# Attention's side work on VectorE: two steps in a unit that also has side work for the array, few in the others

## The chip, the cores and the metric

The kernel runs on one core of a Trainium2 chip. The metric is the device time of one execution in microseconds (us), the median of several runs. TensorE (PE) multiplies matrices into PSUM, VectorE (DVE) does reductions and elementwise work, ScalarE (ACT) exponentials and copies, GpSimd (POOL) elementwise work and indirect transfers, and SyncE (SP) starts most transfers. Each engine works through its own queue in order and waits for the others by semaphores.

## The reference

The input is x of shape (8, 1024, 256). Three layers follow each other, each added to x:

```
x = x + 0.5 * moe(layernorm(x))     # top-1 routing over 8 experts of 320 slots;
                                    # tokens past the slots go through one shared network
x = x + attention(layernorm(x))     # 16 heads of width 16, over 1024 positions
x = x + 0.5 * moe(layernorm(x))
```

Attention, which the change is about, computes for each batch and head

```
xd   = layernorm(x) @ W_down                    # split in 16 heads of 16
q, k, v = xd @ toqueries, xd @ tokeys, xd @ tovalues   (q and k scaled by 16 ** -0.25)
out  = softmax(q @ k.T) @ v                     # 1024 x 1024 scores for each head
x    = x + out @ W_unify + b_unify
```

## The kernel before

**Pairs and units.** The attention loop (`run`, from L1230) goes over 32 pairs n = 4 b + g: batch b of 8 and group g of four heads. A pair has 16 units u, two halves of the queries by eight blocks of keys. A unit is a fixed pattern on four engines:

- TensorE computes the scores of pair n (`psc`, L987, kinds "s" of `ORDERS`) into four PSUM banks and, interleaved with them and on other strips of the array, the scores of the next pair n + 1 the other way round (`pm`, also L987, kinds "m"), which use three PSUM banks.
- ScalarE turns the scores into exponentials (`ex`, L996), four instructions of 512 columns per unit. So the start of every fourth of them marks a unit.
- VectorE reduces each `pm` to its largest value (`halves`, L1003), four instructions per unit. These serve the next pair's softmax. Until a bank is reduced TensorE can't fill it again.
- TensorE multiplies the exponentials of the unit before by the values (`av`, L1018). After eight units VectorE transposes the sums and inverts the denominators (`turned`, `rec`, L1033 and L1036), GpSimd multiplies (`ot`, L1041), and after each second pair VectorE transposes back (`ho`, L1053). This falls into units 0, 1, 8 and 9. At the end of units 7 and 15 VectorE combines the maxima (L939 to L946), and SP carries them on (L948, L949).

**Side work.** Everything else in this stage is written as generators: `prepare(b)` (queries, keys and values of a coming batch: transposes L832, projections L862 and L880, values L894), `unify(b)` (the output projection L1063 and its addition to x, L1071), `stats(b)` (the attention norm of batches 4 to 7: eight pairs of L148 and L149, a closing part L151 to L160, and four Newton iterations L168 to L173, two to a step), `route(b)` (the same norm for the next layer, transposes, router logits L1091 and L1100, the places in the experts' slots in `places` L288 to L346, and eight sends to DRAM L184, L186, L361), and `biased(b)`. Each generator yields the kind of its next piece: `ARRAY`, `DVE` or `POOL`. They stand in a list `beside` with the pair by which they must be finished.

`step(kind)` takes one piece from the generator that is due first among those whose next piece is of this kind. `done_by(n)` at the end of a pair forces what is due by then. The order on TensorE, VectorE and ScalarE is exactly the order in which the Python code issues (`manual_schedule`); GpSimd and SP are ordered by the framework.

**Where pieces are taken.** Within each half of a pair, `SLOTS_OF` names the units (u modulo 8) for array pieces and those for VectorE pieces. In pairs with g of 2 or 3 array pieces are taken in units 0, 1 and 4 and VectorE pieces in 2, 3, 5 and 6; in pairs with g of 0 or 1 array pieces in 0, 1, 3 and 5 and VectorE pieces in 2, 4 and 6. So no unit has both. In a unit with an array piece (`other` is true) the whole `av` product comes before the second group of scores, and GpSimd's piece is left out.

Parts of `places` go back and forth: VectorE copies sums (L236), GpSimd adds three times (L238), VectorE adds (L308), GpSimd multiplies (L310), VectorE reduces (L312), and so on.

`queue(n)` puts new generators on the list at the start of a pair: for n of 1 to 4 also the load of batch 3 + n from DRAM (L74, after a one-element `memset` L1162) with its `stats`.

## Time and profile before

| | |
|---|---|
| median of 3 runs | 2935.99 us (2933.0 to 2938.25) |
| profiled execution | 2939.6 us, its span 2937.9 us |
| first layer, with the first pair's scores, to 662 us of the span | 662 us |
| attention loop | 662 to 2450 us, 1788 us |
| last layer | 2450 to 2938 us |
| busy in the span: TensorE, VectorE, ScalarE, GpSimd | 95%, 64%, 47%, 29% |
| mean granted TensorE clock | 0.981 |
| mean of one L1003, one L996 | 681 ns, 596 ns |

An instruction group in the profile is given as line, engine, operation, what it writes and reads, shapes, count, then its busy time and the mean time of one, then how long its engine had been idle before it and what it waited for. "<-PE pm L987" means that the wait ended when TensorE's `pm` at line 987 was done. In a list of stages the columns after the stage are its length, the busy time of PE, PEld (weight loads), DVE, ACT and POOL with their counts, the granted TensorE clock (1.00 is full), the busy share of the DMA engines and GB/s. In a timeline the columns are start, length, engine, line, operation and count; in brackets stands the idle time before it. Neighbouring instructions of one kind are merged there. The mean of L1003 includes overlap with the next one.

### The profile page before, as it was taken

Reading aid. Unit: us, or ns where it says so; the run is one execution under the profiler, and the core shown is the slowest. Engines: PE = TensorE matmul, PEld = TensorE weight load, DVE = VectorE, ACT = ScalarE, POOL = GpSimd, SP = SyncE. Lnnn points to the kernel's source line nnn. Section 1 sums busy time; section 2 is a strip of 40 time slices with the busy share of each in tenths; the row PEclk is TensorE's granted clock in tenths of the full one; section 3 lists DMA queues with packets and bytes.
Section 4 is the critical chain, followed back from the end, with each engine's and each line's share of the span. In section 5 each row is a group of like instructions: output and inputs, shape, how many; then the busy total and the mean of one; then the engine's idle time right before and its main releaser. Section 6 shows DMA issues by size and latency. Waiting matters only on the chain.

```text
span 2937.9 us, 56693 instructions
## 1 busy us (share of the span) xinstructions
PE 2799.3 (95%) x22066; PEld 1546.2 (53%) x22066; DVE 1883.1 (64%) x4189; ACT 1375.2 (47%) x2512; POOL 851.8 (29%) x1136
## 2 busy tenths in 40 slices
PE   4799999899999999999999999999999999999998
PEld 4567776454444444444444444444444445666775
DVE  7344223467897888888788788788788963212221
ACT  1111111207766666766766765766766663111111
POOL 3434433414001033123222321420420214432331
PEclk7799999999999999999999999999999999999999
DMA  7522553413112101301301301311321102321440
GB/s 224 152 83 78 176 187 99 161 47 121 53 58 97 67 24 60 124 24 56 128 24 52 133 24 42 125 41 39 125 80 38 39 3 73 128 61 49 150 147 28
DMA packets 163737, 251.47 MB, mean 86 GB/s; under 512 B 36737, under 2 KB 109698, under 8 KB 163458
## 3 DMA queue, kind: packets, MB, share of 16 engines
q1 hardware_dynamic: 144178, 196.93, 20.6%
q0 software_dynamic: 18432, 50.62, 5.1%
q8 instruction: 177, 2.90, 0.4%
q14 instruction: 102, 0.84, 0.1%
q10 hardware_dynamic: 848, 0.18, 0.0%
HBM read 144.10 MB, written 103.57 MB: 84 GB/s over the span
## 4 chain that ended last, share of the span: by engine, by line
PE 63%; DVE 13%; issue 1%; DMA 0%; POOL 0%; ACT 0%; POOLq 0%; DVEq 0%
PE psc L987 20%; PE av L1018 15%; DVE halves L1003 9%; PE pm L987 6%; PE pe_o L499 5%; PE ph_o L456 5%; PE pe_e L499 2%; PE ph_e L456 2%; PE pu L1063 2%; PE pxd L862 2%; PE pv L894 1%; DVE turned L1033 1%; PE pq L880 1%; PE pl L1091 1%; PE ptrn L832 0%
## 5 line engine op out<-in xcount | busy, mean ns | idle before, releaser
L1003 DVE TENSOR_REDUCE halves<-pm 128x1 f32<-128x512 f32 x2048 | 1309.3, 681 | 260.9 <-PE pm L987 239.6
L996 ACT ACTIVATE ex<-psc 128x512 f32<-128x512 f32 x2048 | 1111.4, 596 | 574.5 <-PE psc L987 570.9
L987 PE MATMUL pm<-k,q 32*128 32x512 f32 x4096 | 870.5, 448 | 50.6 <-DVE halves L1003 38.6
L987 PE MATMUL psc<-q,k 32*128 32x512 f32 x4096 | 791.8, 455 | 3.1 <-PEq L668 3.1
L1018 PE MATMUL av<-ex,vp 128*32 128x256 f32 (+1 forms) x6472 | 610.9, 449 | 0.0
L987 PEld LDWEIGHTS psc<-q,k 32*128 32x128 f32 x4096 | 326.6, 183 | 479.0 <-issue 423.1
L987 PEld LDWEIGHTS pm<-k,q 32*128 32x128 f32 x4096 | 374.9, 183 | 133.4 <-DVE halves L1003 107.3
L987 PE MATMUL psc<-m,ones_r 32*128 32x512 f32 x2048 | 406.9, 390 | 0.0
L456 PE MATMUL ph_o<-bT_o,oa 128*128 128x512 f32 x704 | 318.6, 601 | 7.1 <-DVE h_o L474 5.3
L499 PE MATMUL pe_o<-ob,h_o 128*128 128x256 f32 x1408 | 322.6, 386 | 0.0
L1041 POOL TENSOR_TENSOR ot<-turned,rec 128x256 f32<-128x256 f32 x64 | 39.7, 620 | 883.9 <-DVE rec L1036 875.6
L499 PEld LDWEIGHTS pe_o<-ob,h_o 128*128 128x128 f32 x1408 | 268.1, 193 | 48.5 <-issue 13.8
L1018 PEld LDWEIGHTS av<-ex,vp 128*32 128x32 f32 x6472 | 127.6, 108 | 298.3 <-issue 275.6
L456 PEld LDWEIGHTS ph_o<-bT_o,oa 128*128 128x128 f32 x704 | 131.2, 191 | 159.7 <-issue 147.4
L470 ACT ACTIVATE h_o<-ph_o,ob 128x512 f32<-128x512 f32 x88 | 60.5, 687 | 328.9 <-PE ph_o L456 305.0
L987 PEld LDWEIGHTS psc<-m,ones_r 32*128 32x128 f32 x2048 | 196.6, 184 | 13.0
L474 DVE TENSOR_SCALAR h_o<-ph_o,ob 128x512 f32<-128x512 f32 x88 | 65.9, 748 | 196.2 <-ACT h_o L470 179.4
L509 DVE SCALAR_TENSOR_TENSOR y_o<-pe_o,old_o 128x256 f32<-128x256 f32 x88 | 37.2, 423 | 205.8 <-PE pe_o L499 141.2
L499 PE MATMUL pe_e<-wb,h_e 128*128 128x256 f32 (+1 forms) x640 | 143.9, 381 | 0.0
L456 PE MATMUL ph_e<-bT_e,wa 128*128 128x320 f32 x512 | 140.6, 433 | 1.8 <-ACT bT_e L204 1.8
L204 ACT COPY bT_o<-pt_bT_o 128x1024 f32<-128x1024 f32 x22 | 22.3, 1012 | 250.8 <-PE pt_bT_o L200 225.9
L499 PEld LDWEIGHTS pe_e<-wb,h_e 128*128 128x128 f32 (+1 forms) x640 | 112.9, 179 | 16.4 <-issue 3.1
(183 smaller groups left out, 2385.1 us busy)
## 6 DMA issues: line engine op xcount, KB each, us to landing
k<-krows SPq DMA_DIRECT2D x64, 512.0 KB
wa<-in_w_dram SPq DMA_DIRECT2D x16, 1024.0 KB
wb<-in_w_dram SPq DMA_DIRECT2D x16, 1024.0 KB
krows<-kh SPq DMA_DIRECT2D x32, 512.0 KB
krows<-kl SPq DMA_DIRECT2D x32, 512.0 KB
q<-qrows SPq DMA_DIRECT2D x32, 512.0 KB
rows_o<-buf SPq DMA_DIRECT2D x88, 130.0 KB
x<-in_x_dram SPq DMA_DIRECT2D x8, 1024.0 KB
```

The source lines that it names most:

```text
L456: nc.tensor.matmul(ps[:, i * 512 : i * 512 + width], lhsT=wa[:, k, (m + i) * P : (m + i + 1) * P], rhs=xnt[:, k, c0:c1], start=(k == 0), s ...
L470: nc.scalar.activation(t[:, 0, : hi - lo], ps[:, lo - c0 : hi - c0], AF.Relu, bias=bias[:, m : m + 1],)
L474: nc.vector.tensor_scalar(t[:, 1, : hi - lo], ps[:, 512 + lo - c0 : 512 + hi - c0], bias[:, m + 1 : m + 2], 0.0, ALU.add, ALU.max,)
L499: nc.tensor.matmul(ps[lo - i * P : hi - i * P, :D], lhsT=of[:, lo - a : hi - a], rhs=w[:, m, :], start=(m == 0), stop=(m == MC - 1),)
L509: nc.vector.scalar_tensor_tensor(y[:n, :], ps[:n, :D], 0.5, olds[i][:n, :], ALU.mult, ALU.add)
L862: nc.tensor.matmul(ps, lhsT=wd_sb[:, k, m * P : (m + 1) * P], rhs=xnt[:, k, :], start=(k == 0), stop=(k == KC - 1),)
L987: nc.tensor.matmul(ps, lhsT=lhs, rhs=rhs, start=(len(left) + 1 == todo[kind, h, "of"]), stop=not left,)
L996: nc.scalar.activation(ex, ps, AF.Exp, scale=S ** -0.5)
L1003: nc.vector.tensor_reduce(halves[m][:, t, half, h : h + 1], ps, AX.X, ALU.max, negate=True)
L1018: nc.tensor.matmul(avs[n, q][32 * h : 32 * h + 32, cols], lhsT=vps[b % 2][:, at : at + 2 * S], rhs=ex[:, cols], start=(c == 0), stop=(c == ...
L1041: nc.gpsimd.tensor_tensor(outs_t[q][:, :, at : at + S].rearrange("p (t a) s -> p a t s", t=4), by[:, :, :S].rearrange("p (a t) s -> p a t ...
L1063: nc.tensor.matmul(ps[:, i * D : (i + 1) * D], lhsT=outs[b, g, q][:, at : at + P], rhs=wu_sb[:, g, :], start=(g == 0), stop=(g == G // 2 - 1),
```

## The change

`SLOTS_OF` keeps only the units for array pieces, unchanged. The units for VectorE pieces are no longer listed. Where an array piece is taken in a unit, two VectorE pieces are taken right after it. In the other units one VectorE piece is taken only in the seventh of each half (u modulo 8 of 6), and in the last pair, which has no next pair, in each odd unit.

```diff
-        SLOTS_OF = [((0, 1, 4), (2, 3, 5, 6)), ((0, 1, 3, 5), (2, 4, 6))]
+        SLOTS_OF = [(0, 1, 4), (0, 1, 3, 5)]
...
-                        other = u % TB in slots[0] and due(ARRAY) is not None
+                        other = u % TB in slots and due(ARRAY) is not None
...
-                    if u % TB in slots[1]:
+
+                    if other:
+                        step(DVE)
+                        step(DVE)
+                    elif u % TB == TB - 2 or not ahead and u % 2:
                         step(DVE)
                     if not other:
                         step(POOL)
```

An array piece counts as taken also where the generator only ends there and issues no matmul. The order of the pieces within a generator is the same as before, and so are all instructions.

## The prediction

> **What bounds the kernel now.** I read the page first (busy shares, costliest groups), then the busy time by stage, then who waited for whom in attention, then VectorE's timeline at the places that the change touches.

> ```profile
> PE 2799.3 (95%) x22066; PEld 1546.2 (53%) x22066; DVE 1883.1 (64%) x4189; ACT 1375.2 (47%) x2512; POOL 851.8 (29%) x1136
> ...
> L1003 DVE TENSOR_REDUCE halves<-pm 128x1 f32<-128x512 f32 x2048 | 1309.3, 681 | 260.9 <-PE pm L987 239.6
> ```
> ```profile
> 662.00:2450.00 1788.00, 1746.50 (x17698) 808.71 (x17693) 1462.77 (x2894) 1207.10 (x2244) 426.89 (x527) 1.00 0.19 65
> ```
> ```profile
> DVE halves L1003 <- PE pm L987: 214.1, 471, 4.0
> ...
> PEld pm L987 <- DVE halves L1003: 92.1, 145, 1.3
> ```
> Attention is 1788 us: TensorE is busy 1746 of them, VectorE 1463. VectorE waits 214 us for TensorE's scores and TensorE's weight loads wait 92 us for VectorE's reductions, so TensorE leads and VectorE follows so closely that any lump on it shows. 92 us is more than this change could give back, since the fixed work of units 0, 1, 8 and 9 causes part of it.

> A unit's length is the distance between the starts of every fourth `ex` (L996). The plain unit, with neither array work nor a step, is 2.94 us. VectorE's four reductions start 0.605 us apart, so they fill 2.42 of it and leave 0.26 behind each pair of them.

> **What a step costs today.** A half iteration is three Newton operations (L168, L169, L173), and a step holds two halves:
> ```profile
> 1242.12 1.29 DVE L1003 TENSOR_REDUCE halves<-pm 128x1 f32<-128x512 f32 x2 [0.17 <-PE pm L987]
> ...
> 1246.39 0.16 DVE L168 TENSOR_TENSOR a_f<-yi_f 128x8 f32<-128x8 f32 x1
> ...
> 1247.38 0.17 DVE L173 SCALAR_TENSOR_TENSOR yn_f<-a_f,yn_f 128x8 f32<-128x8 f32 x1
> 1247.47 2.58 DVE L1003 TENSOR_REDUCE halves<-pm 128x1 f32<-128x512 f32 x4
> ```
> ```profile
> 1245.48 1.09 ACT L996 ACTIVATE ex<-psc 128x512 f32<-128x512 f32 x2 [0.54 <-PE psc L987]
> ...
> 1249.07 1.09 ACT L996 ACTIVATE ex<-psc 128x512 f32<-128x512 f32 x2 [1.07 <-PE psc L987]
> ```
> The six operations hold VectorE 1.08 us, and the unit that the step runs into lasts 1249.07 - 1245.48 = 3.59 us instead of 2.94: some 0.63 lost. A statistics step (L148, L149) holds it 0.55 and costs 0.09. Both fit one rule, an estimate: loss = holding - cover - 0.20, where the cover of a plain unit is 0.26 and 0.20 is the lead that TensorE has through its three `pm` banks.

> In a unit with array work, the cover, VectorE's idle time before the next reduction, is 1.53 us (projection, L862, L880), 1.59 (values, L894), 0.91 (transposes, L832), 0.5 (router logits, L1091), 1.0 (projection in unit 0 or 8). It is nothing with `unify`, whose own addition waits for the matmuls:
> ```profile
> 1564.52 0.69 DVE L1071 TENSOR_TENSOR x<-x,pu 128x512 f32<-128x512 f32 x1 [0.44 <-PE pu L1063]
> 1565.13 0.20 DVE L946 STREAM_TRANSPOSE lowturned<-lowboth 128x32 f32<-128x32 f32 x1
> 1565.26 1.24 DVE L1003 TENSOR_REDUCE halves<-pm 128x1 f32<-128x512 f32 x2
> ```

> **The change, part by part.** I wrote out from the code which step falls into which unit, before and after. No instruction is added; the order moves.

> *Routes 0 to 5.* Before, a route is spread over pairs 4k+1 to 4k+4. After, its statistics fall two at a time into units 0, 1, 3, 5 of pair 4k+1 (score and value projections, transposes), both Newton steps into unit 8, transposes and logits into pair 4k+2, the slot chain into units 0 and 1 of pair 4k+3. Taken away per route: two Newton steps at 0.63, four statistics at 0.09: 1.6 us. Placed: two statistics hold 1.1, under the idle times above: 0. Two Newton steps hold 2.16 in unit 8 with a cover of 1.09: 2.16 - 1.09 - 0.20 = 0.87. `top` to `chosen` in one unit waits for POOL's L293 (0.32, with hand-overs 0.5): 0.39 + 0.5 + 0.39 held, 0.58 covered: 0.5. The last step before them, alone: 0.1. The chain:
> ```profile
> 1776.76 0.20 DVE L236 COPY sums<-places 128x56 f32<-128x56 f32 x1
> 1778.19 0.22 DVE L308 TENSOR_TENSOR place<-sums,places 128x64 f32<-128x64 f32 x1 [1.23 <-POOL sums L238]
> ```
> VectorE is held 1.6 us here with POOL's three additions. Then POOL's L310 (0.65 with hand-overs), L312 to L316 (0.5) and L321 (0.25) follow in the same unit 0: 3.0 in all; unit 1 gets 1.2 + 0.63 for `behind` and the slots. With the division's work (1.2) and eight reductions (4.84) VectorE needs 10.8 for two units in which TensorE has 7.0. They take about 10.7. Spread as before they cost 9.35 (units 0 and 1: 6.82; added by the two array steps and what follows: 1.62 and 0.91). Price 1.4. In return the transposes in units 0 and 8 cover the division's delay (3.63 instead of 2.94 there): -0.8. Per route -1.6 + 0.87 + 0.5 + 0.1 + 1.4 - 0.8, with up to 0.2 because a prepare step sits one slot earlier, is +0.5; six routes: +3.

> *Norms of batches 4 to 7 (`stats`).* Taken away: 7.0 us (units 3.0 to 3.7 long in pairs 1, 2, 3, 6, 7, 10). Placed: pair 4 has `unify`, so nothing covers: two statistics 0.95 and (behind `ho`) 1.1, final step and Newton 1.37, Newton and statistics 1.36; unit 8, where the generator only ends, 1.1; 0.7 after: 6.6. Pair 1, unit 8 also has no matmul: 2.3 for two Newton steps. Pairs 5 and 6: 0.7 and 2.6 (logits with two Newton steps and the 0.7 of `ho`). Single steps elsewhere: 0.4. Together 12.6.

> Then a wait that did not exist. The load of batch 4 is issued at 720.39 on SP, behind two loads of `k` and one of `q`; before, its first reader came at 731.78:
> ```profile
> 722.40 1.22 DVE L1003 TENSOR_REDUCE halves<-pm 128x1 f32<-128x512 f32 x2
> 723.53 0.20 DVE L946 STREAM_TRANSPOSE lowturned<-lowboth 128x32 f32<-128x32 f32 x1
> 724.39 1.29 DVE L1003 TENSOR_REDUCE halves<-pm 128x1 f32<-128x512 f32 x2 [0.65 <-PE pm L987]
> ...
> 731.78 0.42 DVE L148 BATCH_NORM_STATS2 st_a<-x 128x6 f32<-128x256 f32 x1
> ```
> After, it stands at 723.6 at the head of VectorE's queue, with L946, the pair's reductions and so TensorE behind it (and SP's L948, `krows` behind L946; their readers are eight units away). The trace's packets of this load end at 728.11, its semaphore seems complete at 728.4. [...] I take 5.0. Stats net: 12.6 + 5.0 - 7.0 = +10.6.

> *Route 6 and the end.* Before, its Newton steps and transposes lie in pairs 29 to 31 and only slots and sends are left at 2450. After, it gets four steps by pair 30, the rest in pair 31, where VectorE is nearly idle; transposes come in the last unit. Taken away: 4 us. Left over, one behind the other: copies, POOL's second rows (4 x 1.22), transposes, logits, two POOL hand-overs, slots: 16.8 us against 5. Upper end 12. The lower end is about 0: at the border of the sections TensorE took L200 of the next layer ahead of the last `pu` groups, so part may be filled. I take 8: net +4.

> *POOL.* Sends (1.22 + 0.19 + 1.1) move to units 2 to 9 of pair 4k+3, one per 2.94: tight, `ot` may come 2 us late; `ho` is read a unit later. Zero; up to 0.5 per route if not.

> *Clock.*
> ```profile
> 1775.50:1779.10 3.60, 3.45 (x33) 1.62 (x28) 2.32 (x6) 2.17 (x4) 1.56 (x5) 1.00 0.00 0
> 1779.10:1782.50 3.40, 3.40 (x25) 1.51 (x25) 2.27 (x6) 1.09 (x2) 0.20 (x1) 0.50 0.00 0
> ```
> A slot chain is followed by 3.4 us at half clock; that unit took 5.10 instead of 3.61. It happened twice in attention. [...] I take 4.

> Sum: 3 + 10.6 + 4 + 4 = 21.6, bounds +1 to +40. The profiled execution took 2939.6 (span 2937.9), 3.6 above the median 2935.99; the gain or loss is set on the median: 2957.

> **The rivals.** *Faster (9%):* the idle times do cover, because VectorE's lag is carried over several units instead of stopping TensorE. For it: 1.5 us in some 30 units. Then takings of 1.6 x 6 + 7 + 4 = 20.6 remain against the load wait and half the rest, 9: 2924. It decides at a lead of about a microsecond; against it stands 0.09 for a 0.55 us step, a lead of 0.20. *No change (9%):* the order does not do what it says in most batches. In pairs 4k from 8 on there are seven array units and no VectorE step is ready. If then the end is filled and no clock window falls, about +4: 2940. *Far slower (20%):* end wholly exposed, eight half-clock windows, late `ot`: 2936 + 36 = 2972. *Forecast (62%):* 2942 to 2966, 2957 likeliest.

> A difference of 0.2%, 5.9 us, is about what a measurement of this kernel can tell from none. The range leaves out most of the two upper rivals' far ends: 2936 to 2975. Slower 0.82, within 0.09, faster 0.09.

> **What would show it.** Right: a wait of L148 for the load of `x` near 724 of 4 to 6 us; pair 4 at 66 us instead of 59.9; units 0 and 1 of pair 4k+3 together near 10.7; pairs 2, 3 and 30 shorter by 1.6 to 2.6; a gap on TensorE after 2450. Wrong: weight loads waiting for L1003 well under 92 us in all, or no load wait. Pairs 4k+1 longer than 61 us would mean that the lead is smaller than I read.

## The result and the profile after

The kernel after takes 3003.52 us (median; 2999.3 to 3006.52), the kernel before 2937.12 with the runs made beside it: ratio 1.0226, 95% interval 1.0209 to 1.0244. The change costs 66 us. The direction was forecast, the size (21 us) was not, and the time lies above the range.

The page of after first: busy time, share and instructions of each engine, then VectorE's group of reductions (busy, mean ns, idle time before them).

```profile
PE 2850.3 (95%) x22122; PEld 1573.7 (52%) x22122; DVE 1894.5 (63%) x4189; ACT 1374.9 (46%) x2512; POOL 851.9 (28%) x1136
...
L1003 DVE TENSOR_REDUCE halves<-pm 128x1 f32<-128x512 f32 x2048 | 1312.0, 682 | 292.8 <-PE pm L987 279.4
```

VectorE works as long as before (1895 against 1883 us), but TensorE is busy 51 us longer with the same matrices (its count is higher because the trace of before lacks 56 more of their records). That is the first hint: TensorE ran slower for part of the time. Next the two stages, after the first layer (window; then busy us of PE, PEld, DVE, ACT and POOL; granted clock, DMA share, GB/s):

```profile
664.20:2498.00 1833.80, 1777.50 (x17686) 817.78 (x17687) 1471.94 (x2881) 1203.04 (x2237) 418.74 (x512) 0.98 0.18 63
2498.00:3003.00 505.00, 482.98 (x1965) 340.20 (x1957) 125.20 (x316) 73.32 (x121) 177.60 (x241) 0.97 0.29 91
```

The mean clock in attention fell from 1.00 to 0.98. And within attention (waits of one line for another: us in total, times, longest):

```profile
DVE halves L1003 <- PE pm L987: 254.3, 651, 2.9
PEld pm L987 <- DVE halves L1003: 113.3, 166, 4.5
```

Both waits grew, VectorE's by 40 us and TensorE's by 21: VectorE is still the follower, and each has become the other's obstacle more often. Units are compared by the starts of every fourth `ex`. From the first `ex` to the last the loop lasts 1786.5 us before and 1835.0 after; what follows it lasts 489.2 and 503.6. TensorE's time at half clock within the loop is 11.0 us before and 85.3 after.

**The forecast wait for the load of `x`** (VectorE's timeline, start and length; in brackets the idle time and its releaser):

```profile
727.54 1.22 DVE L1003 TENSOR_REDUCE halves<-pm 128x1 f32<-128x512 f32 x2
733.40 0.43 DVE L148 BATCH_NORM_STATS2 st_a<-x 128x6 f32<-128x256 f32 x1 [4.64 <-DMA x<-after_first]
...
734.49 0.18 DVE L946 STREAM_TRANSPOSE lowturned<-lowboth 128x32 f32<-128x32 f32 x1
```

L946 and with it the reductions stand behind it. The unit lasts 11.49 us instead of 4.67; 6.83 us of half clock follow from 733.6 on.

**A kept bank, which nobody forecast.** In pairs 4k+2 of after, units 2, 3, 10 and 11 last 3.80 us, although no piece is in 2 and 3 but VectorE's usual work. Pair 18, on TensorE, TensorE's weight loads and VectorE:

```profile
1726.74 1.06 PE L1091 MATMUL pl<-rw,Trn 128*128 128x8 f32 x8
1738.14 1.06 PE L1091 MATMUL pl<-rw,Trn 128*128 128x8 f32 x8
```
```profile
1729.87 0.18 PEld L987 LDWEIGHTS pm<-k,q 32*128 32x128 f32 x1 [0.42 <-DVE halves L1003]
1731.77 0.18 PEld L987 LDWEIGHTS pm<-k,q 32*128 32x128 f32 x1 [0.41 <-DVE halves L1003]
1733.67 0.18 PEld L987 LDWEIGHTS pm<-k,q 32*128 32x128 f32 x1 [0.42 <-DVE halves L1003]
```
```profile
1739.24 0.18 DVE L1100 TENSOR_TENSOR logits<-pl,rb 128x32 f32<-128x32 f32 x1
```

The router's products go into `pl`, a bank of the same pool of three that `pm` uses. The first piece writes it at 1726.7, the second at 1738.1, and only L1100 at 1739.2 lets it go. For some 12.5 us `pm` has two banks; each half of a unit lasts 1.90 us instead of 1.47, and the weight loads wait 0.4 us for a reduction each time. Before, the two pieces lay in adjacent units (0 and 1, 8 and 9 of pairs 4k+3): in pair 19 they start 4.2 us apart, and L1100 comes 5.3 us after the first. The order of array pieces changed nowhere in the code; the route is simply ready for them one pair earlier, where the array's units are 0, 1, 4.

**Half clock, here after a slot chain** (pair 23; window, busy times as above, clock):

```profile
2013.60:2017.00 3.40, 2.58 (x24) 1.50 (x28) 2.63 (x6) 1.08 (x2) 0.81 (x5) 1.00 0.05 9
2017.00:2027.30 10.30, 10.11 (x72) 3.93 (x69) 5.63 (x12) 4.34 (x8) 8.26 (x12) 0.50 0.14 48
```

Three windows of 3.41 us at half clock follow one in which TensorE was without a recorded product for only 0.8 us. The granted clock recorded in this trace is 1.0 or 0.5, and all its changes, from 126.05 to 2993.25 us, lie on one grid of 3.41333 us, to within 0.002 us; in the trace of before, from 24.64 to 2929.38 us, they lie on one of the same spacing, to within 0.001 us. The loop has eleven stretches at half clock, of one to four windows: 10.2 us at its start (pair 0; before 4.1), 6.8 behind the wait for the load, 13.6 behind Newton steps of the attention norms (pairs 1, 4 and 6), 20.5 behind pieces of the router's products (pairs 6, 10 and 14) and 34.1 behind slot chains (pairs 15, 23 and 27). Behind the slot chains of pairs 7, 11 and 19 there is none.

**The end.** Route 6 finishes alone (VectorE's timeline):

```profile
2509.38 0.19 DVE L1100 TENSOR_TENSOR logits<-pl,rb 128x32 f32<-128x32 f32 x1 [3.40 <-PE pl L1091]
...
2513.37 0.22 DVE L308 TENSOR_TENSOR place<-sums,places 128x64 f32<-128x64 f32 x1 [1.22 <-POOL sums L238]
...
2517.16 0.17 DVE L343 TENSOR_TENSOR slot<-row,behind 128x8 int32<-128x8 f32 x1 [0.32 <-POOL behind L342]
```

The first product of the next layer's experts (`ph_o`) starts at 2520.5, before at 2456.1. That is 64.4 us later, of which 50.5 are already there at the end of the loop.

### The profile page after: what moved, and what is told of

Read it like the earlier page. It is cut to its first block, busy times and chain, and to the rows that moved or that the text cites. A ratio compares the mean times of both kernels' runs of the same rounds, so it can differ in the third digit from the quotient of the medians.

```text
span 3002.8 us, 56812 instructions
## 1 busy us (share of the span) xinstructions
PE 2850.3 (95%) x22122; PEld 1573.7 (52%) x22122; DVE 1894.5 (63%) x4189; ACT 1374.9 (46%) x2512; POOL 851.9 (28%) x1136
## 4 chain that ended last, share of the span: by engine, by line
PE 61%; DVE 14%; issue 1%; POOL 1%; DMA 1%; ACT 0%; POOLq 0%; DVEq 0%; ACTq 0%
PE psc L987 20%; PE av L1018 14%; DVE halves L1003 9%; PE pm L987 5%; PE pe_o L499 5%; PE ph_o L456 5%; PE pe_e L499 2%; PE ph_e L456 2%; PE pu L1063 2%; PE pxd L862 1%; PE pv L894 1%; PE pq L880 1%; DVE turned L1033 1%; PE pl L1091 1%; PE ptan L832 0%
## 5 line engine op out<-in xcount | busy, mean ns | idle before, releaser
L1003 DVE TENSOR_REDUCE halves<-pm 128x1 f32<-128x512 f32 x2048 | 1312.0, 682 | 292.8 <-PE pm L987 279.4
L996 ACT ACTIVATE ex<-psc 128x512 f32<-128x512 f32 x2048 | 1111.3, 596 | 622.7 <-PE psc L987 620.4
L987 PE MATMUL pm<-k,q 32*128 32x512 f32 x4096 | 882.3, 455 | 65.2 <-DVE halves L1003 50.5
L987 PE MATMUL psc<-q,k 32*128 32x512 f32 x4096 | 810.8, 461 | 3.0 <-PEq L668 3.0
L1018 PE MATMUL av<-ex,vp 128*32 128x256 f32 (+1 forms) x6528 | 623.4, 454 | 0.0
L987 PEld LDWEIGHTS psc<-q,k 32*128 32x128 f32 x4096 | 331.4, 186 | 497.0 <-issue 412.8
L987 PEld LDWEIGHTS pm<-k,q 32*128 32x128 f32 x4096 | 378.4, 187 | 147.5 <-DVE halves L1003 128.6
L987 PE MATMUL psc<-m,ones_r 32*128 32x512 f32 x2048 | 412.9, 395 | 0.0
L987 PEld LDWEIGHTS psc<-m,ones_r 32*128 32x128 f32 x2048 | 200.4, 188 | 13.8
```

What stands on the lines that cost most here:

```text
L987: nc.tensor.matmul(ps, lhsT=lhs, rhs=rhs, start=(len(left) + 1 == todo[kind, h, "of"]), stop=not left,)
L996: nc.scalar.activation(ex, ps, AF.Exp, scale=S ** -0.5)
L1003: nc.vector.tensor_reduce(halves[m][:, t, half, h : h + 1], ps, AX.X, ALU.max, negate=True)
L1018: nc.tensor.matmul(avs[n, q][32 * h : 32 * h + 32, cols], lhsT=vps[b % 2][:, at : at + 2 * S], rhs=ex[:, cols], start=(c == 0), stop=(c == ...
```

## The experiments

Times are medians; ratios, with their 95% intervals, are to the kernel before on the same chip (medians of 2936.5 to 2941.8), and can differ by 0.2% from the quotient of two medians. "Half" is TensorE's time at half clock within the loop (11.0 before, 85.3 after), in the one execution that was profiled. Executions of one kernel differ by up to some 25 us (before_wide: 2958.09 to 2983.39), so a single value of it says little about a few microseconds of the median. A unit or pair is said to be at full clock when no half clock lies in it.

### One cause at a time

**The slot chain spread again: one VectorE step instead of two in pairs 4k+3** (after_chain_apart)

```diff
                     if other:
                         step(DVE)
-                        step(DVE)
+                        if n % G != 3:
+                            step(DVE)
```

> The changed kernel with one VectorE step instead of two in array units of pairs 4k+3 only, so that L321 and the second array piece of the slot chain go to units 6 and 8. Theory 2, the chain of slot steps through VectorE and GpSimd in one unit stops TensorE long enough that the clock is halved for some 10 us: units 0 to 2 of pairs 4k+3 fall from 13.5 us together to about 11.5 and what leaves comes back partly in unit 8; the half-clock windows in pairs 4k+3 and just before go away: 3003.5 to about 2985. Rival 2, the clock windows come from elsewhere (the kept bank in pairs 4k+2, or chance): gain of at most 6, windows as many as before (75 us of the loop).

2982.54, ratio 1.0155 (1.0131 to 1.0179): 21 us better than after. Pairs 4k+3 last 52.6 us (53.2 at full clock in after), only some 4 us in all; half fell to 39.3. Between the profiled executions the loop is 18.9 us shorter, most of it clock; the first layer, which the edit does not touch, is 7.0 shorter too.

**No step in units 0 to 2 of pair 1** (after_load_first), so that nothing asks for the `x` of batch 4 before it has come

```diff
                     if other:
-                        step(DVE)
-                        step(DVE)
+                        if n != 1 or u > 2:
+                            step(DVE)
+                            step(DVE)
```

> The changed kernel without VectorE steps in units 0 to 2 of pair 1, so that no statistics stand at the head of VectorE's queue before batch 4 has come from DRAM. Theory 4: the wait of 4.64 us and the half-clock time behind it (10 us) leave pair 1, which goes from 65.3 to 57 to 58 us; pair 4 and later pairs take on the steps that are put off, within 2 us: 3003.5 to about 2996. Rival 4: the stop of TensorE in pair 1 has another cause, pair 1 stays above 62.

2996.4, ratio 1.0179 (1.0155 to 1.0203). Pair 1 lasts 56.2 us, without half clock, instead of 65.3: the load wait cost 9 there, of which its own 4.64 us are half. The loop as a whole was only 1.5 us shorter in the profiled execution (the slowest of four), since other pairs had more half clock (half 89.3).

**The kernel before's VectorE slots from pair 28 on** (after_end_old)

```diff
-                    if other:
+                    if n >= (B - 1) * G:
+                        if u % TB in ((2, 3, 5, 6), (2, 4, 6))[n % G < 2]:
+                            step(DVE)
+                    elif other:
...
```

> The changed kernel with the VectorE slots of the kernel before in the last four pairs (28 to 31), the new rule elsewhere. Theory 3, the end: route 6 is no longer left for after the loop; the stretch from the loop's end to the kernel's end is 490 us again instead of 505, pairs 28 to 31 lose their gain of 5.5: 3003.5 to about 2994. Rival 3: the 14 us behind the loop are clock or chance: no change beyond 3.

2985.64, ratio 1.0175 (1.0131 to 1.0218): 18 us better than after, where 10 were expected. What follows the loop lasts 489.4 instead of 503.6, with 8.3 us of half clock in it instead of 26.6. So the late end is real and worth some 14 us, part of it clock; the rest of the 18 is not the end's (in the profiled execution the untouched first layer is 4.8 shorter).

**The logits read later in the kernel before: a bank kept without any other change** (before_logits_late)

```diff
+                for _ in range(2 - q):
+                    yield DVE
                 nc.vector.tensor_tensor(
                     logits[:, 4 * q : 4 * q + 4, :],
...
-                yield ARRAY if q == 0 else DVE
+                if q == 0:
+                    yield ARRAY
```

> The kernel before with only the reading of `pl` (L1100) put off: for the first four rows by two VectorE slots (from unit 1 to unit 3 of pairs 4k+3), for the second by one (unit 9 to 10, together with L289 and L291). No steps in pairs of two, no other piece moves. Theory 1, the kept bank: units 2, 3 and 10 become 3.80 instead of 2.92 us, 2.6 us a route, six routes in the loop 15.6: about 2952. Rival 1: a late reader costs nothing but two empty steps: 2937 within 2.

2962.84, ratio 1.0076 (1.005 to 1.0102). Units 2, 3 and 10 of pairs 4k+3 last 3.80 instead of 2.92, as forecast; half rises to 21.1, which was not expected and makes 3 to 4 of the 11 us above the expectation; some 6 lie outside the loop and are not explained. The kept bank alone costs 0.86 us a unit, in a kernel that is otherwise before.

### The kept bank taken away, and the gain that did not come

**All of the router's products in the first piece** (after_pl_whole), **or all in the second** (after_pl_together)

```diff
-                    if i == 1:
-                        yield
```
```diff
+                yield
                 pl = bank_v(f"pl_{b}_{q}")
...
-                    if i == 1:
-                        yield
```

> The changed kernel with both halves of the router logits (L1091) of four rows in one array piece, so that the PSUM bank `pl` is not kept from one array piece to the next. Theory 1, the kept bank: in the changed kernel `pl` is written in units 1 and 9 of pairs 4k+2 and released only in units 4 and 12, and TensorE has two `pm` banks instead of three meanwhile; units 2, 3, 10 and 11 then go back from 3.80 to about 2.94 us, pairs 4k+2 lose 3.6 us or more, six routes 22 us: 3003.5 to about 2979. Rival 1, VectorE lags from the steps taken two at a time, or GpSimd's adds and row norms slow VectorE: units 2, 3, 10, 11 stay near 3.8 and the time stays within 3 us of 3003.

> The changed kernel with the first of the two array pieces of the router logits left empty and all eight products in the second, so that every piece keeps its unit and only the time that `pl` is kept shrinks. Theory 1, the kept bank: units 2, 3, 10 and 11 of pairs 4k+2 fall from 3.80 to 2.94 us, units 4 and 12 grow by what the products take (under 0.9); pairs 4k+2 from 56.9 to about 53.5 us where no half clock falls into them, 6 x 3.4 = 20 us: 3003.5 to about 2983, give or take 8 for the clock. Rival 1 (lag of VectorE, or GpSimd beside it): pairs 4k+2 stay above 56.

3002.13 (1.0218; 1.019 to 1.0247) and 3005.93 (1.0197; 1.0165 to 1.0228). No gain. Yet the units did what was expected: 2 and 3 are back at 2.94 in the one, pair 22 is at 54.2 us in the other. Instead half rose to 119.5 and 123.5. In after_pl_whole the slot chain also moves, into pairs 4k+2, of which those from 10 on hold 13 to 27 us of half clock each; in after_pl_together pairs 4k+3 with their slot chain hold 6 to 14.

**Twelve products of 384 columns (not used) behind each of the slot chain's two groups of products, added to after_pl_whole** (whole_filled), to keep TensorE streaming there

```diff
             nc.tensor.matmul(total, lhsT=ones_r, rhs=chosen, start=True, stop=True)
+            for _ in range(12):        # and the same behind the products of "behind"
+                nc.tensor.matmul(ps[:, 128:512]..., lhsT=ones_r, rhs=ones_r..., ...)
```

> As after_pl_whole (both halves of the router logits in one piece), and besides twelve matmuls of 384 columns that nobody reads behind the matmuls of `places` and twelve behind those of `behind` (L304 to L331), so that TensorE has 2 us of work in each of the two places where it waits for the slot chain; their output is not used. Theory 2, halted TensorE halves the clock: the half-clock time in the attention loop falls from 119 us to under 50 and the kernel gets faster by 15 to 25 us although it does more work: about 2980. Rival 2, the clock does not follow the halts in the chain: half-clock time stays near 119 us and the time stays at 3002 or grows by up to 2 x 2 us a route, 3002 to 3026.

3024.14 (1.0273; 1.0247 to 1.03). They lengthened the chain more than they filled it; half fell only from 119.5 to 90.4. This decides nothing.

### What brings half clock

**One or two reductions of 2048 elements on VectorE (not used), in ten plain units of the kernel before** (before_hold_2: one; before_hold_4: two)

```diff
+                    if n % G == 0 and 8 <= n < 28 and u % TB == 6:
+                        for i in range(1):        # 2 in before_hold_4
+                            hold = small.tile([P, 8], F32, tag="hold", ...)
+                            nc.vector.tensor_reduce(
+                                hold, bu_sb.unsqueeze(1).to_broadcast([P, 8, D]), AX.X, ALU.max
+                            )
                     last = (n, u, [todo["ex", h] for h in range(4)])
```

> The kernel before with one reduction of 2048 elements of SBUF on VectorE (result not used) in units 6 and 14 of pairs 8, 12, 16, 20 and 24, which had neither array work nor a step: ten halts. The reduction holds VectorE about 2.1 us, so by holding less cover (0.26) less lead (0.20) each costs 1.65: 16 us in all, 2953, with pairs 4k at 62.5. If a halt of TensorE also brings half clock, 3.4 us or more of it follow each halt, and the pairs with it are longer by 0.35 of its time: 3.4 us at each would add 12 us, 10 us at each 35 us. If it does not, the loop stays at 11 us of half clock.

> As the kernel with one reduction, with two of them in each place: VectorE is held about 4.2 us, and by holding less cover less lead each halt costs 3.75: 38 us in all, 2975, pairs 4k at 66.8. TensorE then stands still for more than one window of 3.4 us, so half clock is to follow nearly every halt: ten times 3.4 to 10 us, 12 to 35 us more. If the length of a halt decides, this kernel shows far more half clock than the one with one reduction; if only the phase decides, about the same.

2972.21 (1.0101; 1.0066 to 1.0136) and 3009.55 (1.0233; 1.0201 to 1.0264). The reduction holds VectorE 2.28 us. In before_hold_2 two of the five pairs show no half clock: they are 4.5 and 3.6 us longer, 1.8 to 2.2 for each hold, and the prediction's rule (holding less 0.26 less 0.20) gives 1.82. The other three have 4.9, 8.2 and 10.9 us of half clock and are 5.3, 6.5 and 7.8 us longer. Less the mean 4.02 that leaves 0.27, 0.31 and 0.35 us lost for each us of half clock (0.33 to 0.35 with the half clock that runs over into the next pair). In before_hold_4 all ten holds are followed by it.

Which halts it follows is seen when the time is cut in windows of 3.41 us, counted from a change of the clock. Twice the same hold (before_hold_2, pairs 12 and 8; columns as above):

```profile
1368.57:1371.98 3.41, 1.93 (x26) 0.99 (x25) 3.40 (x5) 1.26 (x3) 0.00 (x0) 1.00 0.00 0
1371.98:1375.39 3.41, 3.41 (x23) 1.04 (x20) 2.43 (x8) 1.25 (x3) 0.00 (x0) 0.50 0.00 0
```
```profile
1133.06:1136.47 3.41, 2.68 (x32) 1.03 (x29) 3.35 (x5) 2.17 (x4) 0.00 (x0) 1.00 0.08 25
1136.47:1139.88 3.41, 2.12 (x25) 0.99 (x25) 3.36 (x7) 1.09 (x2) 0.00 (x0) 1.00 0.01 2
1139.88:1143.29 3.41, 2.67 (x30) 1.14 (x28) 3.34 (x9) 2.17 (x4) 0.62 (x1) 1.00 0.02 5
```

In pair 12 the halt falls into one window: TensorE streams 1.93 of 3.41 us, and the next window is at half clock. In pair 8 it is shared by neighbours, 2.12 is left, and nothing follows. The six windows of this kernel behind which the holds brought half clock had 1.83 to 2.15 us of busy TensorE; holds that brought none left 2.00 or more. So holds of one length, 2.28 us, differ here by how the windows cut the halt; with two of them in a place, half clock followed at all ten.

**Products of 8 columns against products of 384 columns** (before_narrow, before_wide), in the same ten units, none of them used

```diff
+                    if n % G == 0 and 8 <= n < 28 and u % TB == 6:
+                        fill = bank_v(f"fill_{n}_{u}")
+                        for _ in range(16):       # before_wide: 12
+                            nc.tensor.matmul(fill[:, :8], ...)   # before_wide: 384 columns
```

> The kernel before with 16 products of 8 columns each (result not used) on TensorE in units 6 and 14 of pairs 8, 12, 16, 20 and 24, ten places, as the router's products stream them: some 1.95 us each, 20 us in all. If TensorE counts as busy in them, nothing else changes: 2957 and 11 us of half clock in the loop. If products of 8 columns count as standing still, a window of 3.41 us that holds 1.4 us of them is followed by half clock: some seven of the ten places, 35 us or more of half clock, 12 us more, 2969.

> The same places with 12 products of 384 columns each (result not used), some 2.0 us in each place, 20 us in all. If what counts is what TensorE streams, no half clock follows any of the ten places: 2957 and about 11 us of half clock in the loop. If any disturbance of the order brings half clock, it shows as much of it as the kernel with the narrow products.

3007.07 (1.0227; 1.0209 to 1.0245) and 2969.47 (1.0101; 1.0069 to 1.0133). The narrow ones came out longer than meant, 3.7 us and more a place (each product is two instructions), the wide ones 2.36 at the first place. Around the first place, narrow and then wide:

```profile
1130.99:1134.40 3.41, 3.41 (x38) 2.78 (x32) 1.80 (x4) 1.09 (x3) 0.00 (x0) 1.00 0.10 33
1134.40:1141.22 6.82, 6.82 (x47) 4.00 (x46) 2.29 (x4) 1.62 (x4) 0.00 (x0) 0.50 0.01 2
```
```profile
1134.11:1137.52 3.41, 3.41 (x34) 2.64 (x30) 1.46 (x4) 0.73 (x3) 0.00 (x0) 1.00 0.00 0
1137.52:1140.93 3.41, 3.41 (x44) 1.38 (x36) 3.16 (x9) 2.65 (x6) 0.00 (x0) 1.00 0.01 2
```

By the record TensorE is busy throughout in both. Half clock follows all ten places of the narrow products and none of the wide ones (half 102.4 and 24.6; in before_wide it lies in pairs 0 and 11). So half clock follows these products of 8 columns as it follows the halts above. The narrow work was also the longer; but TensorE had no gap in it, so length alone explains nothing. Not separated is whether the few columns matter or the weight load ahead of each of the 32 instructions (12 in the wide ones).

That is part of what ate the gain of the single piece: it puts 1.95 us of such products next to each other. Most of the rest fell behind the slot chain and the work around it. With products of 8 columns left out of the count, half clock followed, over the traces of all 18 kernels, 67 of 75 full-clock windows of the loop in which TensorE was busy under 1.7 us, 69 of 143 with 1.7 to 2.3, 41 of 1963 with 2.3 to 3.3, and none of 7068 with more. Counted as busy, these products would leave 62 windows with more than 3.3 us that half clock followed. Of the 41, 30 hold products of the slot chain: why it follows these at up to 3.3 us of recorded work stays open.

**The two pieces in adjacent units** (after_pl_near): array pieces in units 0, 3, 4 of pairs 4k+2

```diff
-                    slots = SLOTS_OF[n % G < 2]
+                    slots = (0, 3, 4) if n % G == 2 else SLOTS_OF[n % G < 2]
```

> The kernel after, with its array steps in units 0, 3, 4 and 8, 11, 12 of pairs 4k+2 (0, 1, 4 before), so that the two pieces of the router's products come in adjacent units, as in the kernel before, and not in one burst. If the kept bank is the cost, two units less per half of a pair last 3.80 instead of 2.94: pairs 4k+2 from 56.9 to about 53.5 at full clock, 20 us in all, and no half clock is added: 2983. If half clock comes from disturbances of any kind, it rises as it did with the single piece, and the time stays at 3000 or above.

2981.73, ratio 1.0138 (1.0116 to 1.016), near the forecast of 2983, though by another sum: pairs 18, 22 and 26 last 54.1 to 54.3 us instead of 56.8 to 56.9, 2.7 us a pair or 16 in all where 20 were expected, and half falls to 58.6, some 8 us more. Pairs 4k+2 hold only 3.4 us of half clock, in pair 6. So the bank's cost was real, and with the single piece its gain had been spent on the clock.

### Put together

**The four single edits at once** (after_mended: all products in the second piece, one step in pairs 4k+3, no step in units 0 to 2 of pair 1, old slots from pair 28), **and one Newton step instead of two in unit 8** (mended_newton)

```diff
...
+                        if n != 1 or u > 2:
                             step(DVE)
+                            if n % G != 3:        # mended_newton: and not unit 8 of pairs 4k+1
                                 step(DVE)
...
```

> The kernel after with the four edits that were tried one at a time: the router's products in one piece (no score bank is kept), one VectorE step instead of two in pairs 4k+3 (the slot chain apart), the old slots from pair 28 on, and no step in units 0 to 2 of pair 1. If these four are the whole cause, the times by pair at full clock add up to the kernel before: pairs 4k+2 near 54.2, pairs 4k+3 near 52.6, pair 1 at 56.2, what follows the loop at 489, a loop near 1790 with under 25 us at half clock, and 2945. If the half clock comes from any halt and is not bound to these four, it falls elsewhere: 60 us or more of it in the loop, and 2960 to 2975.

> As the kernel with all four edits, and one VectorE step instead of two in unit 8 of pairs 4k+1, so that the second Newton step of a route falls into unit 9. If a Newton step costs by what it holds, unit 9 falls from 5.4 to 4.7 and unit 10 grows by 0.1: some 0.6 us less in each of six or seven pairs, 4 us in all. If it meets GpSimd's subtraction L850 there, a two-input operation L169 or L173 lasts 1.2 us instead of 0.17, unit 10 grows by a microsecond and the time rises by 3 to 6 us against that kernel.

2969.15 (1.0099; 1.0073 to 1.0125) and 2968.46 (1.009; 1.0065 to 1.0115). This was the expectation of the rival: 58.9 and 106.8 us of half clock, most of it in pairs 4k+2, behind the single piece. The profiled executions were the fastest of after_mended (2955.79) and the slowest of mended_newton (2978.84), so the two values of half do not compare the kernels. Splitting the Newton steps makes pairs 4k+1 from 9 on 0.6 us shorter (59.3), as expected; whether that shows in the whole, 4 us expected, can't be told from medians 0.7 apart in runs that spread over 13 and 23 us.

**Steps by what they stand beside** (best1: all products in one piece, the load and end edits; best3: the near pieces instead)

```diff
+                    kind = other and due(ARRAY)[2].__name__
...
+                    elif other and kind == "prepare" and (n != 1 or u > 2):
                         step(DVE)
+                        if n % G != 1 or u != TB:     # best1: if u % TB
                             step(DVE)
+                    elif other and kind == "route" or u % TB == TB - 2:
+                        step(DVE)
```

> The changed kernel with: both halves of the router logits in one piece; two VectorE steps only beside a piece of `prepare` (one in units 0 and 8), one beside a piece of `route`, none beside `unify`; none in units 0 to 2 of pair 1; the VectorE slots of before in the last four pairs. If the four causes (kept bank, halved clock, wait for the load, end) are the whole loss, what is left is the gain of pairs 4k+1 and 4k+3 (some 1.5 us a batch), of pairs 2 and 3 (3 us) and of the clock: about 2926, and under 2937 at the least. If something else of the new order costs, it stays above 2940.

> Array steps in units 0, 3, 4 of pairs 4k+2 as in the kernel with the near pieces; two VectorE steps only beside the preparation of a batch (one in unit 8 of pairs 4k+1), one beside the route, none beside unify; none in units 0 to 2 of pair 1; the old slots from pair 28 on. If kept bank, half clock after bursts and halts, the load wait and the late end are all that the change costs, pair 1 lasts 56, pair 4 60, pairs 4k+1 59.3, 4k+2 53.5, 4k+3 52.6, with under 25 us of half clock in the loop: 2928 to 2942, level with the kernel before. If not, 2955 or more, as the two mended kernels.

best1: 2969.2 (1.0096; 1.0074 to 1.0118), with 67.3 us of half clock, and pairs 4k+1 up to 66 us long. best3: 2936.0 against 2941.32 for before, ratio 0.9977 (0.9965 to 0.9989): a little faster than before, and far faster than after. It keeps two steps in a unit only beside `prepare`, so it is less of the change and not the change with its costs taken away. Half is 24.8, of which 13.7 stand in pair 11. Its loop, from the first `ex` to the last:

```profile
662.00:2447.30 1785.30, 1743.40 (x17640) 811.45 (x17637) 1471.36 (x2893) 1206.77 (x2243) 427.21 (x524) 0.99 0.19 65
```

## Why the prediction was wrong in size

The loop grew by 48.5 us, what follows it by 14.4, and the first layer, which the change does not touch, by 2.0.

- **Half clock, the step that failed most.** The prediction took 4 us, an estimate that no run shows. In its place the trace of after shows 74 us more of it in the loop (85.3 against 11.0), at the mean 0.31 some 23 us; behind the loop 18 us more, 6 us if the loop's price holds there. The price of one window (1.5 us, measured 1.1) was near; the count was not. Behind the holds of before_hold_2 1.26 to 1.58 us without a recorded product in one window of 3.41 us was enough, and one stretch of half clock lasts up to 13.7 us in after. The trace of before already had half clock behind a stretch in which TensorE was busy for 3.45 of 3.60 us, and that row should have had the larger weight. The trace was also misread: only one of its two windows, in pair 19, stands behind a slot chain; the five other chains in pairs 7 to 27 brought none. The other, in pair 15, stands behind the first piece of the router's products (TensorE, then the windows before and at half clock, of the kernel before):

```profile
1506.95 1.06 PE L1091 MATMUL pl<-rw,Trn 128*128 128x8 f32 x8
```
```profile
1506.03:1509.44 3.41, 3.31 (x36) 2.17 (x36) 2.88 (x7) 1.37 (x3) 0.62 (x1) 1.00 0.87 332
1509.44:1512.86 3.42, 3.42 (x20) 1.09 (x12) 1.57 (x3) 1.18 (x3) 0.00 (x0) 0.50 0.06 10
```

  So the hint at the narrow products lay there too, and slot chains alone were not the right count either: after has half clock behind three of them (34 us), behind router pieces (20), norms and load (20).
- **The kept bank, missing in the sum.** Six routes at 2.7 us, 16 us. The prediction moved transposes and logits into pairs 4k+2 and reckoned what the transposes give back there, but not how long the bank stays taken between the two pieces. The list of steps by unit that it was made from shows unit 1 and unit 4; asking who owns the bank in between was left out.
- **The rest was about right.** Of the loop's 48.5 us 9.5 remain after clock and bank; the prediction had 3 + 10.6 for routes and norms and -4 taken away from route 6, 9.6. So close an agreement is partly luck: with 0.27 to 0.35 for a us at half clock the remainder is anything from 6 to 12; pairs 4k+1 from 9 on gave back 1.0 to 1.6 us each, more than reckoned, and the slot chain cost more (units 0, 1 and 2 of pair 7 last 4.23, 5.32 and 4.03 us, together 2.6 more than in pair 27 of before). Behind the loop 14.4 less those 6 leave 8 to 9; forecast were 8.
- **Single forecasts that held.** The load wait is 4.64 us (4 to 6): in after the load's last packet ends at 732.93 and its reader starts 0.47 us later. The 5.0 us that the sum takes for it is an estimate that no run shows; in its place pair 1 is 9 us shorter without the wait (after_load_first, 56.2 instead of 65.3). Pair 4 lasts 66.9 us (66), 3.4 us of it at half clock. Pairs 2, 3 and 30 are shorter by 1.7, 1.7 and 2.5. Two Newton steps in unit 8 make unit 9 last 5.41 instead of 4.68, 0.73 (0.87). The loss rule was measured directly by the holds (1.8 to 2.2 us each, by the rule 1.82). Units 0 and 1 of pair 4k+3 last 9.6 together, not 10.7: the chain runs on into unit 2.
- **The rivals.** "Far slower" was nearest: its exposed end came, but at about the middle price, and its eight windows at half clock were 25 in the loop, in 11 stretches.

## What to carry to other kernels

When steps move, list for each buffer how long it is taken, not only what each step costs: a piece that ends half a step later can keep a bank through units that have nothing to do with it. And where TensorE runs near its full clock, look at what it streams in each 3.41 us: here six windows that a halt had cut to 1.83 to 2.15 us of work (before_hold_2), and all ten bursts of 16 products of 8 columns (before_narrow), were paid a second time as half clock. So keep narrow products apart and lumps on the following engine short. A mended cause that brings no gain may have been the right cause, with its gain spent elsewhere; compare stage lengths at equal clock before it is dropped.

## What was not expected of the hardware

```profile
975.71 0.17 DVE L169 SCALAR_TENSOR_TENSOR a_f<-a_f,v_f 128x8 f32<-128x8 f32 x1
...
976.32 1.24 DVE L169 SCALAR_TENSOR_TENSOR a_f<-a_f,v_f 128x8 f32<-128x8 f32 x1
```
```profile
976.25 1.28 POOL L850 TENSOR_TENSOR ql<-whole,qh 128x512 fp32r<-128x512 f32 x1 [2.63 <-issue]
```

  L169 ends at 977.56, L850 at 977.53. It happened in six pairs of best1 (5, 9, 13, 17, 21 and 25), where both Newton steps lie in unit 9. Whether the one is the cause of the other, no run here isolates.
